# Four edits to a four-layer graph kernel: a copy ahead of its stores, a list spacing, a bias added later, edge sums and rest stores moved

## The chip, the cores and the metric

The kernel runs on one core of a Trainium2 chip. The metric is the time of one execution on the device in microseconds (us), median of three runs. Engines are named as the profile names them: PE (TensorE matmul), PEld (its weight loads), DVE (VectorE), ACT (ScalarE), POOL (GpSimd), SP (SyncE). Each engine carries out its instructions in order, and a DMA is issued by an instruction in the queue of SP, ACT or POOL.

## The reference, cut to what matters

There are 4096 nodes with 256 features and a weighted 4096 x 4096 adjacency, dense in the first rows and columns and thin elsewhere. Four graph layers follow each other, each with a residual and a normalization:

```python
x = layernorm(x + adj @ (x * W))                                   # layer 0
x = layernorm(x + two_steps(x, adj))                               # layer 1
x = layernorm(x + softmax(where(adj != 0, adj * score, -big)) @ x) # layer 2
x = layernorm(x + [x, adj @ x, rowsum(adj * adj.T)] @ weight + bias)  # layer 3
# two_steps: R = (adj + I) / rowsum; twice: A = top-p attention of Xa,
# Xf = R @ Xf, Xa = A @ Xa, Z += Xf @ U1.T + Xa @ U2.T;
# result: layernorm(x + Z) * ln_g + ln_b
```

## The kernel before, in words

A row tile is 128 nodes, so there are 32. The adjacency comes as blocks of 128 x 128. Tiles 0 to 2 are multiplied densely in every layer. For the others layer 0 finds by the way which columns hold anything, and writes a list of them (4 to 7 groups of 128 columns a tile); later layers gather just these rows with indirect DMAs on POOL (L371). In layer 0 itself, tiles 0 to 7 are multiplied densely, and 8 to 31, the 24 listed ones, by their new lists.

**Layer 0** is a loop over slots. In each slot the ends of finished tiles move on by a step (`move_ends`), every second slot multiplies four blocks of a dense tile (`dense_0`, L519, with the maxima that say what is filled, L521), most slots load a quarter of a tile that is to be listed (`find_0`, L528, L531), and then lists and listed products move on by a step each. The order of PE, ACT, DVE and POOL is the order in which the program writes the instructions; SP's own order is left to the scheduler. `list_one` has five steps: counts on DVE (L322 to L325), offsets on PE (L329 to L332, into the bank `lists_ps`), marks on DVE (L338), a product on PE (L342, into the same bank) and the read-out on DVE (L348 to L358). A new list starts at the earliest `APART` slots after the one before.

The end of a tile (`out_0`, seven steps, L447 to L489) normalizes the tile to `xi`, turns it on PE (`xT`), multiplies it for keys and queries (`psq`) and for the residual path (`po`, L442), and then, on ACT, copies keys and queries (`project`, L297 to L302), issues four stores (L475 to L478: `xi` into the tables `tab` and `tak`, and `xb`, which is `xi` plus `ln_b`, made on POOL at L469), copies half of `po` to `qs` (L480) and stores it (L481). `rest` (L485), which DVE does at the end of the slot's dense part, makes `qp` out of the other half of `po` and of `qs`; its store (L489) is the tile's last step.

**Layer 1** has two attention steps over 32 tiles each. Step one follows a written schedule of 15.8 us a tile. Step two has a period of about 32 us a tile; POOL does small operations on one number a row in it, the secant (L757), and gathers for the sums. `out_1` (L1006) ends a tile: load `xb` as `x0` (L1010), scale the sum (L1012), normalize (L1016), times `ln_g` (L1017), plus `x0` (L1018), normalize again (L1023), store `x2`.

**Layer 2** (`product` with `nbr_weights`) goes through 57 chunks: 24 of dense tiles 0 to 2 and 33 pieces of lists, mixed, with the next three chunks of each kind loaded ahead on SP (L1590, L1594). A chunk is weighted on ACT (L1541) and DVE (L1542) and multiplied on PE (L1621). A tile's end, `out_2` (L1646), is spread over the following chunks; it stores y3 on ACT's queue and t3, from a pool of two buffers, on SP's (L1662). Once a chunk the generator `edges_1` (L1560) moves by one `yield`: it loads two 128 x 1024 stretches of `hubs` (512 KB each, L1567) into the upper half of kT, and DVE multiplies them and adds them up (L1569), 12 times in all, for the edge term of tiles 0 to 2. **Layer 3** is the same `product` without weights, reads t3 back (L1672), and adds the edge term in `out_3`.

Of the kernel before, what the change touches and what calls it, by code (L numbers as in the profile page):

```python
# [11 lines left out]
F32 = mybir.dt.float32  # L12
# [6 lines left out]
P = 128  # L19
N = 4096  # L20
D = 256
DA = 64
NT = N // P
# [22 lines left out]
TW = D + DA  # L46
SLOTS = 8
L_EVERY, L_WAIT = 3, 5
F_SLOTS, APART = (6, 7), 3
HB = 8  # L50
NEW = 7
HUBS = (3, 6)
# [22 lines left out]
def gnn_kernel(ctx: ExitStack, tc: tile.TileContext, x, pair, panels, W0, W1, W2T, W3T, U1T, U2T,  # L75
               ln_g, ln_b, Hv, W3L, b3, hubs, out):
    nc = tc.nc
# [5 lines left out]
    dram = ctx.enter_context(tc.tile_pool(name="dram", bufs=1, space=bass.MemoryType.DRAM))  # L83
# [35 lines left out]
    def row_bcast(v, n, name, tag=None):  # L119
        t = const.tile([P, n], F32, name=name, tag=tag or name)  # L120
        nc.gpsimd.dma_start(t, bass.AP(tensor=v.tensor, offset=v.offset, ap=[[0, P], [1, n]]))
        return t

    def one(name, dtype=F32, bufs=2):
        return small.tile([P, 1], dtype, name=name, tag=name, bufs=bufs)

    def rows(I):
        return slice(I * P, (I + 1) * P)
# [3 lines left out]
    w0b, bb = row_bcast(W0, D, "w0b"), row_bcast(ln_b, D, "bb")  # L132
# [104 lines left out]
    def transposed(tiles, name, apart=False):  # L237

        n = 2 * len(tiles)
        pt = bank([P, 4, P], "ptx", "ms")  # L240
        for s, t in enumerate(tiles):
            for h in range(2):
                nc.tensor.transpose(pt[:, 2 * s + h, :], t[:, h * P:(h + 1) * P], ident)
        xT = work.tile([P, 4, P], F32, name=name, tag="xT")
        def turn():
            nc.scalar.copy(xT[:, :n, :], pt[:, :n, :])
        if apart:
            return turn, xT
        turn()
        return xT  # L250
# [23 lines left out]
    def layernorm(o, y, own=True):  # L274
        m, rs = norm_stats(y, own)
        nc.vector.tensor_scalar(o, y, m, rs, op0=OP.subtract, op1=OP.mult)
# [8 lines left out]
    def project(xT, n, I, more=None):  # L285

        half, b = divmod(I, NT // 2)
        r, other = (slice(h * DA, (h + 1) * DA) for h in (half, 1 - half))
        c = rows(n * (NT // 2) + b)
        ps = bank([P, 2, P], "psq", "ms")  # L290
        for h in range(2):
            nc.tensor.matmul(ps[:, 0, :], wqk[:, h, r.start:r.start + P], xT[:, h, :], start=(h == 0), stop=(h == 1))
        if more is not None:
            for h in range(2):
                nc.tensor.matmul(ps[:, 1, :DA], xT[:, h, :], wqk[:, h, :DA], start=(h == 0), stop=(h == 1))
        yield
        nc.scalar.copy(kT[r, c], ps[r, 0, :])  # L297
        q = work.tile([P, P], F32, name="q")
        nc.scalar.copy(q[other, :], ps[other, 0, :])
        (nc.sync if n else nc.scalar).dma_start(qd[n][I], q[other, :])  # L300
        if more is not None:
            nc.scalar.copy(more[:, D:], ps[:, 1, :DA])  # L302

    def run(gen):
        for _ in gen:
            pass
# [110 lines left out]
    tab, tak = (dram.tile([N + P, TW], F32, name=k) for k in ("tab", "tak"))  # L417
    qtab = dram.tile([N, D], F32, name="qtab")
    ttab = dram.tile([N, D], F32, name="ttab")
    qpd, zd, xbd = ([dram.tile([P, D], F32, name=f"{k}_{I}", tag=f"{k}{I}") for I in range(NT)] for k in ("qp", "z", "xb"))  # L420
    x2d = dram.tile([N, D + 2], F32, name="x2d")
    y3d = dram.tile([N, D], F32, name="y3d")
    t3d = dram.tile([N, D], F32, name="t3d")
# [15 lines left out]
    def times_both(xT, u):  # L439
        po = bank([P, 2, D], "po", "ms")  # L440
        for h in range(2):
            nc.tensor.matmul(po.rearrange("p a b -> p (a b)"), xT[:, h, :], u[:, h, :], start=(h == 0), stop=(h == 1))  # L442
        return po
# [3 lines left out]
    def out_0(I, ps, sums, xin):  # L447
        pool = pools["w0"]
        nc.vector.tensor_scalar_add(rone[:, I:I + 1], sums, 1.0)
        nc.vector.reciprocal(rinv[:, I:I + 1], rone[:, I:I + 1])  # L450
        y = pool.tile([P, D], F32, name="y0", bufs=4)
        nc.vector.tensor_mul(y, ps[:, :D], w0b)
        nc.vector.tensor_add(y, y, xin)
        st = small.tile([P, nc.vector.BN_STATS_DIM], F32, name="st")
        nc.vector.bn_stats(st, y)
        mv = small.tile([P, nc.vector.BN_AGGR_DIM], F32, name="mv0", bufs=5)
        nc.vector.bn_aggr(mv, st)
        yield
        rs = one("rs0", bufs=5)
        nc.gpsimd.tensor_scalar_add(rs, mv[:, 1:2], EPS)  # L460
        nc.gpsimd.tensor_tensor(rs, rs, neg_half, OP.pow)
        yield
        xi = pool.tile([P, TW], F32, name="xi", bufs=4)
        nc.vector.tensor_scalar(xi[:, :D], y, mv[:, 0:1], rs, op0=OP.subtract, op1=OP.mult)
        yield
        xT = transposed([xi], "xT0")
        yield
        xb = pool.tile([P, D], F32, name="xb")
        nc.gpsimd.tensor_add(xb, xi[:, :D], bb)  # L469
        qk = project(xT, 0, I, xi)  # L470
        next(qk)
        po = times_both(xT, U[0])
        yield
        run(qk)
        nc.scalar.dma_start(tab[rows(I), :], xi)  # L475
        nc.scalar.dma_start(tak[rows(I), :DA], xi[:, D:])
        nc.scalar.dma_start(tak[rows(I), DA:], xi[:, :D])
        nc.scalar.dma_start(xbd[I], xb)  # L478
        qs = pool.tile([P, D], F32, name="qs")
        nc.scalar.copy(qs, po[:, 1, :])  # L480
        nc.scalar.dma_start(qtab[rows(I), :], qs)  # L481
        qp = pool.tile([P, D], F32, name="qp")

        def rest():
            nc.vector.scalar_tensor_tensor(qp, po[:, 0, :], rone[:, I:I + 1], qs, op0=OP.mult, op1=OP.add)  # L485

        last_of_slot.append(rest)
        yield
        nc.scalar.dma_start(qpd[I], qp)  # L489

    def run_rest():
# [514 lines left out]
    def out_1(a, psa):  # L1006

        I = a["I"]
        x0 = pools["late"].tile([P, D], F32, name="x0")
        nc.sync.dma_start(x0, xbd[I])  # L1010
        h = work.tile([P, D], F32, name="y")
        nc.scalar.activation(h, psa[:, :D], AF.Copy, scale=a["rk"])  # L1012
        yield
        rs, shift = norm_scale(h)
        yield
        nc.scalar.activation(h, h, AF.Identity, scale=rs, bias=shift)  # L1016
        nc.gpsimd.tensor_mul(h, h, gb)  # L1017
        nc.gpsimd.tensor_add(h, h, x0)  # L1018
        yield
        rs, shift = norm_scale(h)  # L1020
        yield
        x2 = pools["late"].tile([P, D + 2], F32, name="x2", tag="o")
        nc.scalar.activation(x2[:, :D], h, AF.Identity, scale=rs, bias=shift)  # L1023
        yield
        nc.vector.scalar_tensor_tensor(h, x2[:, :D], 1.0, hvb, op0=OP.mult, op1=OP.mult, accum_out=x2[:, D + 1:])
        nc.gpsimd.memset(x2[:, D:D + 1], 1.0)
        nc.gpsimd.tensor_copy(scores[:, I:I + 1], x2[:, D + 1:])
        nc.sync.dma_start(x2d[rows(I), :], x2)
# [433 lines left out]
    with tc.manual_schedule(engines=everything):  # L1462
        for I in range(NT + 1):
# [53 lines left out]
            steps(cuts)  # L1517
            run(end)
            end = out_1(at.pop(I), psa) if I < NT else none
            steps(end)  # L1520
            run(cuts)
# [38 lines left out]
    def edges_1():  # L1560

        part = small.tile([P, DENSE, 4], F32, name="part_e", bufs=1)
        half = [kT[:, N // 2:][:, s * CC:(s + 1) * CC] for s in range(2)]
        for I in range(DENSE):
            for c in range(N // CC):
                for t, h in zip(half, hubs):
                    nc.sync.dma_start(t, h[rows(I), c * CC:(c + 1) * CC])  # L1567
                yield
                nc.vector.scalar_tensor_tensor(half[0], half[0], 1.0, half[1], op0=OP.mult, op1=OP.mult,  # L1569
                                               accum_out=part[:, I, c:c + 1])  # L1570
                yield
        nc.vector.tensor_reduce(edge[:, :DENSE], part, AX.X, OP.add)
# [73 lines left out]
    def out_2(I, ps, rk, x2, y3):  # L1646
        y = work.tile([P, D], F32, name="y")
        nc.vector.scalar_tensor_tensor(y, ps[:, :D], rk, x2, op0=OP.mult, op1=OP.add)
        x3 = pools[ends_in[0]].tile([P, D], F32, name="x3", bufs=ends_in[1])
        layernorm(x3, y)  # L1650
        yield
        yield
        turn, xT = transposed([x3], "xT3", True)
        turn()
        yield
        po = times_both(xT, wl)
        yield
        nc.scalar.copy(y3, po[:, 0, :])
        nc.scalar.dma_start(y3d[rows(I), :], y3)
        t3 = pools[ends_in[0]].tile([P, D], F32, name="t3", bufs=-(-ends_in[1] // 2))  # L1660
        nc.vector.tensor_add(t3, x3, po[:, 1, :])
        nc.sync.dma_start(t3d[rows(I), :], t3)  # L1662

    def end_2(I, ps, _):
# [154 lines left out]
```

## Time and profile before

| what | us |
|---|---|
| median of three runs | 2589.42 |
| the three runs | 2587.23 to 2592.84 |
| the profiled execution | 2587.75 |
| its span | 2586.0 |
| busy PE, DVE, POOL, ACT | 2087.2, 2091.6, 1631.2, 1475.9 |
| layer 0 | 0 to about 513 |
| step one | to about 1030 |
| step two | to about 2185 |
| layer 2 | to about 2420 |
| layer 3 | to 2586 |

"Busy" leaves out instructions that only issue a DMA or wait. The profile's table of waits puts idle time of an engine down to what released it. In timelines, each line gives the start, the duration, the engine, the line of the code, the operation, its tiles and sizes, and in brackets the idle time before it with its releaser; ACTq and SPq are the DMA-issuing instructions of ACT and SP.

### The profile page before, as it was taken

The page shows a single profiled execution, that of the slowest core. Times are in us where ns is not written, and L with a number is a line of the kernel's source. Part 1 is how long each engine was busy: PE and PEld are TensorE (multiplying, and loading weights), DVE is VectorE, ACT ScalarE, POOL GpSimd, SP SyncE. Part 2 cuts the span into 40 slices and gives each one's busy share as a digit, 9 for nine tenths or more (in the row PEclk, how much of TensorE's full clock was granted, in tenths as well). Part 3 has the DMA queues.
Part 4 walks back from the last instruction along what each step waited for, and adds up shares of the span by engine and source line. Part 5 has one row for each costly group of instructions (what it writes and reads, how often), then busy time and mean ns, then how long its engine had stood idle before and what let it go on. Part 6 is the DMA issues. An engine that isn't in the chain of part 4 may idle for free.

```text
span 2586.0 us, 36948 instructions
## 1 busy us (share of the span) xinstructions
PE 2087.2 (81%) x10252; PEld 1483.9 (57%) x10252; DVE 2091.6 (81%) x6401; ACT 1475.9 (57%) x2455; POOL 1631.2 (63%) x2720
## 2 busy tenths in 40 slices
PE   4777767689999898869788888888888876679995
PEld 3555445435555555657566666666666665456784
DVE  4788776489999995477799999999999995588587
ACT  0111111168888886557688889999999962234100
POOL 4666544455565656333788887777777773657475
PEclk7888787889999999989899999999999998899997
DMA  9899776435555545645211111111111114987794
GB/s 334 289 309 296 251 250 188 140 107 155 153 161 158 133 129 139 196 131 160 79 58 57 48 45 44 44 43 44 44 45 44 44 57 131 294 248 213 224 299 145
DMA packets 259815, 383.12 MB, mean 148 GB/s; under 512 B 40880, under 2 KB 166336, under 8 KB 259600
## 3 DMA queue, kind: packets, MB, share of 16 engines
q1 hardware_dynamic: 158432, 212.27, 25.5%
q0 software_dynamic: 43664, 124.79, 17.9%
q10 hardware_dynamic: 57504, 43.60, 5.1%
q8 instruction: 84, 1.38, 0.2%
q14 instruction: 131, 1.07, 0.1%
HBM read 321.31 MB, written 59.21 MB: 147 GB/s over the span
## 4 chain that ended last, share of the span: by engine, by line
DVE 25%; PE 16%; ACT 7%; issue 5%; POOL 4%; DMA 3%; SPq 0%; DVEq 0%; ACTq 0%; POOLq 0%
PE acc L1621 5%; PE psa L235 4%; DVE cand L830 4%; DVE e L876 3%; DVE tmp L824 3%; DVE e L872 3%; PE acc L1059 2%; ACT junk L743 2%; DMA kT<-in_hubs 2%; PE lg L633 2%; DVE top L807 2%; DVE rest L809 2%; ACT junk L749 1%; PE pt L224 1%; ACT e L704 1%
## 5 line engine op out<-in xcount | busy, mean ns | idle before, releaser
L235 PE MATMUL psa<-v,eT 128*128 128x256 f32 x2048 | 504.0, 393 | 75.0 <-ACT eT L226 74.5
L235 PEld LDWEIGHTS psa<-v,eT 128*128 128x128 f32 x2048 | 394.6, 197 | 150.5 <-ACT eT L226 96.5
L743 ACT ACTIVATE junk<-e,h 128x4096 bf16<-128x4096 f32 x64 | 237.5, 3710 | 36.8 <-POOL h L723 26.3
L224 PE MATMUL pt<-ident,e 128*128 128x128 f32 x1024 | 157.5, 284 | 100.1 <-DVE e L876 55.1
L749 ACT ACTIVATE junk<-e,h 128x4096 bf16<-128x4096 f32 x62 | 230.8, 3723 | 0.1
L224 PEld LDWEIGHTS pt<-ident,e 128*128 128x128 f32 x1024 | 130.0, 147 | 144.0 <-issue 99.2
L371 POOL DMA_INDIRECT pc<-in_pair,idx_a x130 | 129.0, 992 | 128.4 <-issue 48.6
L830 DVE MAX8 cand<-tmp 128x8 f32<-128x128 f32 x1024 | 203.9, 276 | 1.1
L226 ACT COPY eT<-pt 128x512 f32<-128x512 f32 x256 | 144.9, 588 | 94.2 <-PE pt L224 93.5
L1120 DVE MAX8 cand<-e 128x8 f32<-128x256 f32 x512 | 175.9, 411 | 3.8 <-ACT e L1112 3.6
L371 POOL DMA_INDIRECT xg<-x2d,idx_x x130 | 134.6, 1036 | 69.2 <-PE acc L1621 31.0
L519 PE MATMUL acc<-xw,panel 128*128 128x257 f32 x512 | 156.1, 458 | 25.4 <-DMA panel<-in_panels 14.1
L1150 ACT ACTIVATE marks<-e,mid 128x1024 bf16<-128x1024 f32 x128 | 140.5, 1145 | 39.9 <-DVE mid L1146 35.8
L371 POOL DMA_INDIRECT xg<-ttab,idx_x x130 | 128.7, 990 | 52.8 <-issue 27.5
L371 POOL DMA_INDIRECT xg<-qtab,idx_x x130 | 125.6, 966 | 54.7 <-issue 30.9
L872 DVE SCALAR_TENSOR_TENSOR e<-e,ties 128x1024 f32<-128x1024 f32 x128 | 156.0, 1280 | 3.0 <-DVE ties L868 0.2
L704 ACT ACTIVATE e<-lg 128x1024 f32<-128x1024 f32 x120 | 123.3, 1027 | 52.4 <-PE lg L633 52.4
L824 DVE SCALAR_TENSOR_TENSOR tmp<-e,h 128x2048 f32<-128x2048 f32 x64 | 150.8, 2356 | 2.3
L1109 PE MATMUL lg<-kT,qi 64*128 64x512 f32 x512 | 148.1, 653 | 3.0 <-DVE want L356 2.9
L519 PEld LDWEIGHTS acc<-xw,panel 128*128 128x128 f32 x512 | 116.0, 235 | 58.2 <-issue 32.9
L633 PE MATMUL lg<-kT,qi 64*128 64x512 f32 x480 | 135.5, 641 | 15.6 <-ACT junk L707 15.6
L371 POOL DMA_INDIRECT xg<-y3d,idx_x x111 | 106.6, 960 | 63.7 <-PE acc L1621 41.5
(345 smaller groups left out, 5476.7 us busy)
## 6 DMA issues: line engine op xcount, KB each, us to landing
e<-in_panels SPq DMA_DIRECT2D x96, 512.0 KB
panel<-in_panels SPq DMA_DIRECT2D x136, 256.0 KB
pc<-pk SPq DMA_DIRECT2D x82, 256.0 KB
xg<-ttab SPq DMA_DIRECT2D x96, 128.0 KB
kT<-in_hubs SPq DMA_DIRECT2D x24, 512.0 KB
pc<-in_panels SPq DMA_DIRECT2D x32, 256.0 KB
pc<-pk SPq DMA_DIRECT2D x19, 320.0 KB
tab<-xi ACTq DMA_DIRECT2D x33, 160.0 KB
```

The costliest lines, as they stand in the source:

```text
L224: nc.tensor.transpose(pt[:, k, :], e[:, (g * 4 + k) * P:][:, :P], ident)
L235: nc.tensor.matmul(ps[:, :D], eT[g][:, k, :], rhs[j][:, :D], start=(j == 0), stop=stop and j == NT - 1)
L371: nc.gpsimd.indirect_dma_start(out=o, out_offset=None, in_=src, in_offset=bass.IndirectOffsetOnAxis(ap=idx[:, c], axis=0))
L519: nc.tensor.matmul(ps[:, :D + 1], a[:, k, :], XW[j][:, :D + 1], start=(j == 0), stop=(j == NT - 1))
L633: nc.tensor.matmul(ps[:, h, :], qi[r, :], kT[r, (n * NC + c) * LC:][:, :LC], start=True, stop=True)
L704: nc.scalar.activation(both(e, c), ps, AF.Exp, accum_out=s8[:, c:c + 1])
L743: nc.scalar.activation(junk_tile(), e, AF.Relu, bias=h, scale=-1.0, accum_out=part)
L749: nc.scalar.activation(junk_tile(), e, AF.Sign, bias=h, scale=-1.0, accum_out=below)
L824: nc.vector.scalar_tensor_tensor(w, ec, h, ec, op0=OP.is_lt, op1=OP.mult, accum_out=low[:, c:c + 1])
L830: nc.vector.max(cand[:, c * (NS // 2) + g, :], w[:, g * SEG:(g + 1) * SEG])
L872: nc.vector.scalar_tensor_tensor(eg, eg, ties[:, g:g + 1], eg, op0=OP.is_gt, op1=OP.mult)
L1120: nc.vector.max(a["cand"][:, b, :], a["e"][:, b * SEG0:(b + 1) * SEG0])
```

## The change

In layer 0 ACT copies `qs` straight after the keys and queries, and the stores of `qs` and `xi` follow one step later; `xb` is neither made nor stored, and `APART` goes from 3 to 4. Step two loads `x0` from the first 256 columns of `tab`, whose rows are 320 numbers long, and adds `ln_b` on POOL before the other two POOL operations of that step. In layer 2, `edges_1` waits three chunks instead of one between the loads and the sum, and the store of t3 is issued one step later.

```diff
-F_SLOTS, APART = (6, 7), 3
+F_SLOTS, APART = (6, 7), 4
...
-    qpd, zd, xbd = ([dram.tile([P, D], F32, name=f"{k}_{I}", tag=f"{k}{I}") for I in range(NT)] for k in ("qp", "z", "xb"))
+    qpd, zd = ([dram.tile([P, D], F32, name=f"{k}_{I}", tag=f"{k}{I}") for I in range(NT)] for k in ("qp", "z"))
...
-        xb = pool.tile([P, D], F32, name="xb")
-        nc.gpsimd.tensor_add(xb, xi[:, :D], bb)
         qk = project(xT, 0, I, xi)
         next(qk)
         po = times_both(xT, U[0])
         yield
+        qs = pool.tile([P, D], F32, name="qs")
         run(qk)
+        nc.scalar.copy(qs, po[:, 1, :])
+        qp = pool.tile([P, D], F32, name="qp")
+
+        def rest():
+            nc.vector.scalar_tensor_tensor(qp, po[:, 0, :], rone[:, I:I + 1], qs, op0=OP.mult, op1=OP.add)
+
+        last_of_slot.append(rest)
+        yield
+        nc.scalar.dma_start(qtab[rows(I), :], qs)
         nc.scalar.dma_start(tab[rows(I), :], xi)
         nc.scalar.dma_start(tak[rows(I), :DA], xi[:, D:])
         nc.scalar.dma_start(tak[rows(I), DA:], xi[:, :D])
-        nc.scalar.dma_start(xbd[I], xb)
-        qs = pool.tile([P, D], F32, name="qs")
-        nc.scalar.copy(qs, po[:, 1, :])
-        nc.scalar.dma_start(qtab[rows(I), :], qs)
-        qp = pool.tile([P, D], F32, name="qp")
-
-        def rest():
-            nc.vector.scalar_tensor_tensor(qp, po[:, 0, :], rone[:, I:I + 1], qs, op0=OP.mult, op1=OP.add)
-
-        last_of_slot.append(rest)
-        yield
         nc.scalar.dma_start(qpd[I], qp)
...
-        nc.sync.dma_start(x0, xbd[I])
+        nc.sync.dma_start(x0, tab[rows(I), :D])
...
         nc.scalar.activation(h, h, AF.Identity, scale=rs, bias=shift)
+        nc.gpsimd.tensor_add(x0, x0, bb)
         nc.gpsimd.tensor_mul(h, h, gb)
         nc.gpsimd.tensor_add(h, h, x0)
...
                     nc.sync.dma_start(t, h[rows(I), c * CC:(c + 1) * CC])
-                yield
+                for _ in range(3):
+                    yield
                 nc.vector.scalar_tensor_tensor(half[0], half[0], 1.0, half[1], op0=OP.mult, op1=OP.mult,
                                                accum_out=part[:, I, c:c + 1])
...
         nc.vector.tensor_add(t3, x3, po[:, 1, :])
+        yield
         nc.sync.dma_start(t3d[rows(I), :], t3)
```

## The prediction, made before the changed kernel was run

> **What bounds the kernel now.** First the busy times by stage (window; then its length; busy us and count for PE, PE weight load, DVE, ACT, POOL; granted PE clock; DMA share; GB/s). The windows are layer 0 to 505 us, attention step two from 1135 to 2150, layer 2 in two halves, layer 3.
>
> ```profile
> 0.00:505.00 505.00, 343.66 (x1439) 245.88 (x1439) 355.92 (x870) 57.71 (x238) 273.02 (x458) 0.83 0.82 261
> 1135.00:2150.00 1015.00, 852.93 (x4012) 640.36 (x4010) 923.24 (x2600) 854.41 (x1054) 763.10 (x1580) 0.97 0.20 61
> 2190.00:2300.00 110.00, 75.99 (x258) 53.50 (x259) 71.16 (x217) 38.36 (x123) 71.20 (x68) 0.85 0.89 284
> 2300.00:2410.00 110.00, 101.71 (x386) 70.41 (x385) 92.16 (x327) 49.98 (x162) 63.43 (x62) 0.97 0.73 210
> 2410.00:2586.00 176.00, 141.85 (x615) 117.73 (x613) 129.62 (x473) 1.86 (x5) 106.60 (x111) 0.93 0.71 225
> ```
>
> No engine is full in layer 0; step two is DVE's (91%); the first half of layer 2 does less PE work than the second in the same 110 us, with DMA at 0.89. Next, DVE alone in layer 0:
>
> ```profile
> 60.00:260.00 200.00, 161.77 (x389) 0.87 0.92 300
> 260.00:510.00 250.00, 168.24 (x428) 0.81 0.68 209
> ```
>
> To 260 us DMA (0.92) sets the pace. After that it does not (0.68), and DVE works 168 of 250 us. The waits of that part say where the rest is (engine, line, what it waited for; us, times, longest):
>
> ```profile
> DVE qp L485 <- ACT qs L480: 35.4, 17, 4.9
> DVE rone L449 <- PE acc L566: 32.3, 10, 6.3
> PE lists_ps L329 <- DVE want L356: 17.6, 4, 6.4
> ```
>
> DVE works or waits nearly all of these 250 us (168 + 71), so it is the engine to free. The timeline of one tile's end shows its longest wait being made: ScalarE issues four stores ahead of the copy that DVE stands still for.
>
> ```profile
> 336.27 0.35 ACTq L475 DMA_DIRECT2D tab<-xi  x1
> 336.66 0.44 ACTq L476 DMA_DIRECT2D tak<-xi  x1
> 337.14 0.46 ACTq L477 DMA_DIRECT2D tak<-xi  x1
> 337.70 0.39 ACTq L478 DMA_DIRECT2D xb<-xb  x1
> 338.13 0.37 ACT L480 COPY qs<-po 128x256 f32<-128x256 f32 x1 [1.89 <-DMA tak<-xi]
> 338.53 0.48 DVE L485 SCALAR_TENSOR_TENSOR qp<-po,rone,qs 128x256 f32<-128x256 f32 x1 [1.67 <-ACT qs L480]
> ```
>
> In layer 2 (waits, 2195 to 2300 us) DVE waits for the loads of the edge sums, and PE for the weights that DVE makes behind them:
>
> ```profile
> DVE kT L1569 <- DMA kT<-in_hubs: 26.4, 8, 6.8
> PEld acc L1621 <- DVE pe L1542: 35.9, 12, 7.0
> ```
>
> The chain that ended last agrees: from 2197 to 2286 us most of it is these loads, 5.7 to 8.4 us each, some 50 us in all. Last, step two around the place of the new addition:
>
> ```profile
> 1915.10 0.73 POOL L1017 TENSOR_TENSOR y<-y,gb 128x256 f32<-128x256 f32 x1
> 1921.97 0.25 POOL L848 TENSOR_SCALAR ud<-f_u 128x1 f32<-128x1 f32 x1
> 1924.06 0.29 DVE L868 TENSOR_SCALAR ties<-ties,ud,f_u 128x4 f32<-128x4 f32 x1
> ```
>
> **What the Trainium skill says.** PSUM — Partial Sum Buffer, on bank collisions: accesses of two engines have to be kept apart by bank, not by address. The trace agrees: L329 writes another part of the bank that L356 reads, and waits. DMA: Bandwidth & Descriptors, "Issuing engines are not separate DMA queues": all queues share 16 engines, so a store taken out on ACT's queue is room for SP's loads; here DMA is at 0.92 to 260 us. TensorE: Matmul & The Clock Gate, Part 1: an idle window of about 3.4 us halves the clock, work restores it. In layer 2 eight matmuls take 3.37 us after a 6.7 us wait and 2.00 us otherwise; a removed wait gives a little more than itself.
>
> **The change part by part.** Sums are against the profiled execution, 2587.75 us (span 2586.0, 1.75 around it), which is 1.67 below the median 2589.42.
>
> *Copy ahead of the stores.* From the end of L302 to the copy lie four issues, 1.9 us above, 2.0 at the median tile. I read all 32 tiles: each gains the smaller of DVE's wait and the time by which the copy can start earlier (the later of L302 and PE's po); where po is last, as at 511.9 us, it gains nothing. Out of 50.9 us (24 waits in layer 0) about 31 go. Part of this turns into waits for PE (the 32.3 us above) and for gathers: I count half, -15; ends 5 and 31. The stores now stand at the head of the tile's next step on ACT, whose 58 us of work in 505 leave room; the copy of xT of a later tile can lie up to 2 us behind them, PE waits there already (25 us), which is part of the halving.
>
> *xb left out.* 32 POOL additions of 0.74 us go (24 us, and 9.6 us in which POOL stood still for xi ahead of its gathers), and 32 stores of 131 KB. 13 of these lie before 260 us: 1.7 MB at 300 GB/s is 5.7 us. I take -4, between 0 and -9.
>
> *APART 4.* Counting slots by the loop's rules: both versions take 135. At a spacing of 3 a list's offset matmuls fall into the slot in which the list before it is read out of the same bank, 10 times, at 4 never. The trace has 18.8 us of such waits in 5 cases, with all of PE's queue behind them. But at 4 the next list's counts share a slot with that read-out 19 times instead of 5, and PE waits for counts already (L324, 4.4 us). A third counts: -6, between +5 and -19. Layer 0 together: -25.
>
> *Addition in step two.* 32 POOL additions at 0.73 us (L1017's duration) = 23 us, in POOL's queue ahead of L1017; the x0 load has the same bytes and is issued some 30 us ahead of its use (1916.65 for the next tile). POOL then runs gathers and L848, which DVE needs at L868: 1.84 us of slack above, 1.1 left. Tiles 3 to 6 have two or three gathers more, 1.25 us each, and POOL works without a break: their periods are 33.6 to 34.9 us instead of 32.0. There it counts in full, with one more tile at the edge: 5 x 0.75 = +4; ends 0 and +12 (half of all tiles).
>
> *Edge sums.* A piece took two slots and takes four, 48 of 57 slots. Now 24 slots last 103 us (2195 to 2298), 4.3 each, and the other 33 last 112, 3.4 each. Without the load wait the first part needs PE 75, DVE 63 + gaps, gathers 66 x 1.25 = 83, DMA (30 - 6.3 MB) at 300 GB/s = 79 us; at 91 us it gains 12. The second part takes over 6 sums of 1.31 us on DVE, which is at 92 of 110: +8 if DVE is its bound, 0 if PE; I take +4. Together -8, between -22 and +6. A load has three slots (10 us) for its 7, so no such wait stays.
>
> *Rest stores one slot later.* The same 32 stores on SP, now behind a slot's loads. SP stops waiting for t3 ahead of loads that are three chunks early: 0. The price is that t3 has two buffers: the next-but-one t3 comes 5.8 to 7.2 us after it where ends are close, while the store would be issued some 3.5 us later and land in 2.9 to 4.7. Four ends of 30 are two slots apart, ten three: at most 4 x 3 + 10 x 1 = +20, at least 0; SP's order is not written by hand, so it may not move. I take 0.
>
> Layer 3: nothing. Sum: -25 + 4 - 8 = -29, so 2558.75 profiled, 2560 as a median.
>
> **Rivals.** *Waits only change places in layer 0*: DVE then waits for L566, PE for xT and counts. For: PE has some 80 us of waits there. Against: DVE is hardly ever free. Layer 0 gives -8, the rest -4: 2577. *All of it counts*: -31 - 19 - 9 in layer 0, -18 in layer 2, +4: 2516 at the far end, a likelier 2534. *t3's buffers, slower*: if SP's queue holds the stores back behind loads that wait for buffers (SP's waits for DVE ahead of L1590 and L1594 come to over 100 us), DVE stands still at L1661 in nearly every end. From 1.0 us each (29 / 28 ends) the change gains nothing; at 1.5 us it is +42, 2602. Against: three of four ends are three slots or more apart. *It doesn't do what it says*: SP orders its own queue, and the hub loads may be issued no earlier against the sums; with layer 0 failing as well, no change, 2588.
>
> **Chances.** Forecast 0.58 (2543 to 2575), waits change places 0.17 (2575 to 2584), all counts 0.09 (below 2543), no change 0.06, slower by t3 0.10. The range 2540 to 2584 holds the first two and a third of the next, near 0.8. A measurement of this kernel tells 0.2%, some 5 us, from none: faster 0.84, within 0.06, slower 0.10.
>
> **What would show it.** Right: the wait of L485 for L480 falls from 51 us to about 20; L329's wait for L356 is gone; layer 0 ends near 488 instead of 513 us; L1569 no longer waits for in_hubs and its last sum comes near 2370 us of the old clock; L868's wait for L848 grows in a few early tiles only. Wrong: L449's wait for L566 grows by what L485 loses; L1661 waits for t3d; step two's period leaves 32.0 us.

## The result, and the profile after

| | before | after |
|---|---|---|
| median of four runs, us | 2588.32 | 2555.83 |
| range, us | 2584.34 to 2592.84 | 2554.81 to 2561.94 |
| span of the profiled execution, us | 2586.0 | 2553.7 |

The ratio is 0.9879, with a 95% interval of 0.9856 to 0.9902: 32.5 us faster, where 29 were forecast. To see where the gain comes from, I took the length of each stage from both traces, each stage ending where the last store of its kind is issued (step one: where ACT copies the last `v`):

| stage, ending with | before, us | after, us | difference | forecast |
|---|---|---|---|---|
| layer 0 (`qp`) | 512.8 | 489.6 | -23.2 | -25 |
| step one (`v`) | 524.8 | 522.0 | -2.8 | 0 |
| step two (`x2`) | 1152.0 | 1159.4 | +7.4 | +4 |
| layer 2 (t3) | 230.8 | 221.6 | -9.2 | -8 |
| layer 3 (out) | 159.3 | 156.4 | -2.9 | 0 |

Kernels whose code is the same up to the end of layer 0 differ there by 4.5 and 6.8 us between traces (489.6 and 494.1; 489.5 and 496.3; these kernels come below). So step one and layer 3 show nothing that could be told from no change.

The windows of the profile after, cut at about the same places of the work as in the prediction, have the same columns (window, length, busy us and count of PE, PE weight load, DVE, ACT and POOL, granted PE clock, DMA share, GB/s):

```profile
0.00:490.00 490.00, 344.09 (x1458) 242.12 (x1458) 350.78 (x879) 57.02 (x244) 249.59 (x427) 0.85 0.81 262
260.00:490.00 230.00, 160.28 (x690) 112.86 (x689) 158.24 (x421) 28.63 (x126) 106.60 (x164) 0.84 0.67 211
1115.00:2130.00 1015.00, 848.43 (x3986) 636.15 (x3984) 922.32 (x2596) 852.31 (x1048) 811.66 (x1609) 0.96 0.20 60
```

Layer 0 holds about the same PE and DVE work in 15 us less, and POOL has lost 23 us there (273 to 250), as foreseen. The part behind 260 us is 20 us shorter with the same DMA share. In step two POOL is 49 us busier in this window, of which the additions are 21.8 (30 by 0.727). The rest is in the spans of its operations on one number a row, whose counts are the same; I don't read work from those.

The waits of the second part of layer 0 after (engine, line, what it waited for; us, times, longest) answer to the three lines of the prediction. Lines have moved: L478 was L485, L474 was L480, L563 was L566.

```profile
DVE rone L449 <- PE acc L563: 40.4, 9, 7.7
PE lists_ps L342 <- DVE since L338: 27.6, 12, 2.6
DVE qp L478 <- ACT qs L474: 20.8, 12, 4.8
PE lists_ps L329 <- DVE upto L324: 6.8, 3, 3.3
```

PE no longer waits for the read-out of a list (`want`, L356), and DVE's wait for `qs` fell from 35.4 to 20.8 us; over the whole of layer 0 from 50.9 to 24.9. But DVE's wait for PE at L449 grew from 32.3 to 40.4 (whole layer: 46.9 to 59.4), and PE's for the marks of a list, L338, over the whole layer from 17.8 to 36.1. Taken together, PE's idle time ahead of L329 and L342, the two places where it waits for a list, is 44.6 us before and 44.6 after. So on this chip PE's waits for lists did change places.

DVE's time shows what was gained. Over layer 0 (512.8 and 489.6 us) it was busy for 357.6 us before and 350.4 after, and idle for 155.2 and 139.2. Of the 23.2 us, 16.0 are thus less waiting, and in the other 7.2 DVE does the same work in less time; where these come from is seen below with `xb`.

The timeline of a tile's end (start, duration, engine, line, operation) shows the edit at work: L474 runs at L302's heels, and the stores come behind it.

```profile
318.62 0.21 ACT L302 COPY xi<-psq 128x64 f32<-128x64 f32 x1 [2.92 <-DMA q<-q]
318.73 0.38 ACT L474 COPY qs<-po 128x256 f32<-128x256 f32 x1
...
319.14 0.48 DVE L478 SCALAR_TENSOR_TENSOR qp<-po,rone,qs 128x256 f32<-128x256 f32 x1 [2.74 <-ACT qs L474]
319.53 0.54 ACTq L482 DMA_DIRECT2D qtab<-qs  x1
```

DVE still waits 2.74 us here, no longer for stores, but because ACT itself came late to L302 and what stands ahead of it.

Step two, at one of the tiles with few gathers; `x` is the buffer of `x0`, and L1014 is the new addition:

```profile
1903.61 0.25 POOL L845 TENSOR_SCALAR ud<-f_u 128x1 f32<-128x1 f32 x1
1904.92 0.29 DVE L865 TENSOR_SCALAR ties<-ties,ud,f_u 128x4 f32<-128x4 f32 x1
1927.90 0.73 POOL L1014 TENSOR_TENSOR x<-x,bb 128x256 f32<-128x256 f32 x1
```

From the end of L845 to DVE's need of it are 1.06 us, where 1.84 were before the change: the addition took its 0.73 out of the slack, and DVE does not wait in such a tile. In early tiles it does. DVE's waits in step two, and one of these tiles:

```profile
DVE ties L865 <- POOL ud L845: 26.4, 9, 16.2
```
```profile
1286.72 0.29 DVE L865 TENSOR_SCALAR ties<-ties,ud,f_u 128x4 f32<-128x4 f32 x1 [1.62 <-POOL ud L845]
```

Before it was 22.7 us in 6 waits. In layer 2 the sums no longer wait for their loads (26.4 us before). A small wait of DVE is new there:

```profile
DVE t L1660 <- DMA t3d<-t: 3.9, 2, 2.5
```

It is the one the prediction named as a sign against itself: a t3 waits for the store of the last but one before it, whose buffer it takes.

### The profile page after: what moved, and what is told of

It is laid out like the page before. It is cut to its first block, busy times and chain, and to the rows that moved or that the text cites. A ratio compares the mean times of both kernels' runs of the same rounds, so it can differ in the third digit from the quotient of the medians.

```text
span 2553.7 us, 36818 instructions
## 1 busy us (share of the span) xinstructions
PE 2083.9 (82%) x10252; PEld 1475.9 (58%) x10252; DVE 2085.3 (82%) x6401; ACT 1475.6 (58%) x2455; POOL 1653.3 (65%) x2720
## 3 DMA queue, kind: packets, MB, share of 16 engines
q14 instruction: 130, 1.06, 0.1%
## 4 chain that ended last, share of the span: by engine, by line
DVE 33%; PE 13%; issue 4%; POOL 4%; ACT 4%; DMA 2%; DVEq 0%; SPq 0%; ACTq 0%; POOLq 0%
DVE cand L827 5%; PE psa L235 4%; DVE e L873 4%; DVE tmp L821 4%; DVE e L869 3%; PE acc L1620 3%; PE acc L1057 2%; DVE top L804 2%; DVE rest L806 2%; DVE vt L267 1%; PE pt L224 1%; ACT junk L740 1%; PE lg L630 1%; POOL xg L371 1%; DMA t3d<-t 1%
## 5 line engine op out<-in xcount | busy, mean ns | idle before, releaser
L516 PE MATMUL acc<-xw,panel 128*128 128x257 f32 x512 | 148.5, 441 | 25.0 <-DMA panel<-in_panels 13.2
L701 ACT ACTIVATE e<-lg 128x1024 f32<-128x1024 f32 x120 | 123.0, 1025 | 48.9 <-PE lg L630 48.8
L1110 ACT ACTIVATE e<-lg 128x1024 f32<-128x1024 f32 x128 | 130.5, 1020 | 29.2 <-PE lg L1107 28.5
```

The costliest lines, as they stand in the source:

```text
L516: nc.tensor.matmul(ps[:, :D + 1], a[:, k, :], XW[j][:, :D + 1], start=(j == 0), stop=(j == NT - 1))
```

## The experiments

The theory to test was the prediction's: layer 0 gains by the copy (most), the spacing and `xb`; step two pays for five tiles; layer 2 gains by the edge sums, and the later store of t3 is free. The rivals were that the waits of layer 0 only change places, and that the late t3 store costs time.

The experiments ran on three chips, each beside the kernel before, and the chips are not alike. The kernel before took 2910.1 us on chip A (all kernels named `only_`), 2890.75 on chip B (`undo_apart`, `undo_copy`, `undo_t3`, `split_add`) and 2589.28 on chip C (`undo_xb`, `rest_last`, `best`, `best_rest`). The runs shown above, with 2588.32, are like those of chip C; whether it is the same chip is not known, and "the faster chip" means both. On A and B step one takes 754 to 780 us instead of 525, with DVE idle and no local engine as releaser (the trace of `only_edges` puts 108 us down to "remote" at one line). What makes it so was not found. Step two lasts about the same there (1154.0 on A, with its code as before), layer 0 537.4 instead of 512.8, layer 3 186 to 189 instead of 159. So stage lengths are compared below, within a chip where nothing else is said. There is one trace of each kernel.

### Layer 0: each edit alone

`only_copy`: the copy ahead, with all the stores, that of `xb` too, one step later.

```diff
-        nc.scalar.dma_start(tab[rows(I), :], xi)
-        nc.scalar.dma_start(tak[rows(I), :DA], xi[:, D:])
-        nc.scalar.dma_start(tak[rows(I), DA:], xi[:, :D])
-        nc.scalar.dma_start(xbd[I], xb)
         nc.scalar.copy(qs, po[:, 1, :])
-        nc.scalar.dma_start(qtab[rows(I), :], qs)
...
         yield
+        nc.scalar.dma_start(qtab[rows(I), :], qs)
+        nc.scalar.dma_start(tab[rows(I), :], xi)
...
```

> The kernel before with the copy of qs ahead of its stores alone; the stores, that of xb among them, go out one step later. If a removed wait of DVE counts by half, layer 0 (512.8 us before, its last qp store) ends 15 us earlier and the whole is 15 us shorter. If waits only change places, layer 0 gains under 5 us and DVE's wait for PE at L449 (46.9 us) grows by what its wait for qs loses (50.9 before). Either way the wait for qs falls to some 20 us and later stages keep their lengths within 2 us.

`only_apart`:

```diff
-F_SLOTS, APART = (6, 7), 3
+F_SLOTS, APART = (6, 7), 4
```

> The kernel before with a list spacing of 4 slots alone. If PE's waits for the shared bank lie on the path by a third, layer 0 is 6 us shorter; L329's wait for L356 (18.8 us) goes to 0. If the waits only move to the next list's counts (L324, 4.4 us before), layer 0 changes by less than 3 us and that wait grows by 10 or more.

`only_xb`: the addition moved to step two and the store left out, nothing else.

```diff
-        nc.gpsimd.tensor_add(xb, xi[:, :D], bb)
-        nc.scalar.dma_start(xbd[I], xb)
...
-        nc.sync.dma_start(x0, xbd[I])
+        nc.sync.dma_start(x0, tab[rows(I), :D])
+        nc.gpsimd.tensor_add(x0, x0, bb)
```

> The kernel before with xb left out of layer 0 and ln_b added on POOL in step two. Forecast: layer 0 4 us shorter (32 stores and 24 us of POOL work less; the copy of qs also loses one of the four issues ahead of it), step two 6 to 7 us longer in its first nine tiles, where POOL has no idle time, so about +3 in all. If the gain of layer 0 came mainly from bytes on the DMA engines and from POOL, layer 0 is 12 us shorter or more.

`only_edges`: the edge sums alone; its layer 0 is that of the kernel before, so it is also the layer 0 that the others are held against.

```diff
-                yield
+                for _ in range(3):
+                    yield
```

> The kernel before with three chunks instead of one between the loads of the edge sums and the sum. If the whole of the gain of layer 2 is this edit, its chunks are 9 to 12 us shorter in all: the first 24 some 21 us faster, the other 33 slower by some 9 (six sums of 1.3 us on a busy DVE), and a bit better than with t3 stored later, whose buffer waits (3.9 us) are absent. If the store of t3 has a part in it, the gain is under 5 us.

| kernel | median, us | ratio (95%) | layer 0, us | against 537.4 | forecast | DVE busy, idle there |
|---|---|---|---|---|---|---|
| `only_copy` | 2888.65 | 0.9925 (0.9906 to 0.9943) | 522.2 | -15.2 | -15 | 357.7, 164.5 |
| `only_apart` | 2890.55 | 0.9926 (0.9907 to 0.9945) | 514.0 | -23.4 | -6 | 354.3, 159.7 |
| `only_xb` | 2913.08 | 1.0009 (0.9990 to 1.0027) | 527.1 | -10.3 | -4 | 350.4, 176.7 |
| `only_edges` | 2902.64 | 0.9973 (0.9958 to 0.9987) | 537.4 | | | 359.3, 178.1 |

In layer 0 the copy gave what was forecast, and the spacing, the change of a single digit, four times its forecast. In the medians of all runs the two are alike, 21.5 and 19.6 us below the kernel before. Here are waits in layer 0 of `only_edges`, then of `only_copy`, then of `only_apart`:

```profile
PE lists_ps L329 <- DVE want L356: 23.8, 7, 6.4
DVE qp L485 <- ACT qs L480: 40.2, 18, 6.1
```
```profile
DVE qp L480 <- ACT qs L476: 21.3, 12, 5.8
```
```profile
PE lists_ps L329 <- DVE upto L324: 5.9, 5, 2.1
```

The copy halves its own wait and hardly touches the other (20.0 us are left of the 23.8). In `only_apart` the wait for `want` is gone. The prediction had reckoned that two thirds of it would come back as waits for counts; that wait (L324) is 5.9 us, hardly more than the 4.4 of the trace it was read from. Yet half of it did come back, elsewhere: PE's idle time ahead of L342 is 44.1 us instead of 31.7. That the stage lost 23.4 us, about what the wait took, is thus no proof that the wait counted in full. These are all of layer 0 in `only_edges` and in `only_apart`:

```profile
0.00:537.40 537.40, 361.86 (x1458) 255.58 (x1458) 359.26 (x874) 59.61 (x244) 271.58 (x459) 0.80 0.77 247
0.00:514.00 514.00, 343.06 (x1458) 243.40 (x1458) 354.28 (x874) 59.56 (x244) 274.66 (x459) 0.83 0.80 258
```

PE's idle time fell by 5 us only (175.5 to 170.9); its same 1458 matmuls took 19 us less, at a granted clock of 0.83 instead of 0.80. DVE's idle time fell by 18 us. So the spacing spares DVE waits and PE slow work, but by what path the one digit does it is not shown.

`xb` gains 10.3 us in layer 0, and 8.9 of them are DVE's own work, which is the same 874 instructions. The cause shows in the single instructions: beside an addition for `xb` on POOL an instruction of DVE takes longer. L464, which makes `xi`, before and after (shortest, median and longest of 32 in ns):

```profile
L464 DVE TENSOR_SCALAR xi<-y,mv,rs x32: 380/406/999, 71.8 to 504.7; 128x256 f32<-128x256 f32 x32
L464 DVE TENSOR_SCALAR xi<-y,mv,rs x32: 381/406/568, 70.1 to 480.8; 128x256 f32<-128x256 f32 x32
```

The longest, 999 ns at 400.88 us, overlaps the addition that starts at 401.63. In all, the 60 DVE instructions that overlap these additions before take 6.1 us more than the median of their kind. In the five traces with `xb` in layer 0 DVE is busy for 354.3 to 359.3 us there, in the nine without it for 350.0 to 351.3. Step two shows no such thing: the 84 DVE instructions that overlap the new additions there take no longer than their median. Which instructions are slowed, and why, is open.

Step two gives 4.3 us of the 10.3 back (1158.3 against 1154.0). The two stages would leave a gain of 6 us, but over all its runs the total of that kernel is that of the kernel before.

### Layer 0: one edit taken back

`undo_apart` is the changed kernel with `APART` at 3; `undo_copy` has the stores ahead of the copy again; `undo_xb` makes and stores `xb` in layer 0 and has no addition in step two.

> The changed kernel with the list spacing back at 3 slots. Alone, the spacing gave 21 us of the whole and the copy 22, the two together with xb left out no more than 23 in layer 0 of the changed kernel. If the two free the same stretches (DVE and PE stand still in turn in the same slots), layer 0 is only 4 to 10 us longer than in the changed kernel of this call (undo_t3, split_add). If each is worth in company what it is worth alone, it is 20 us longer. L329's wait for the list's read-out is back at about 20 us.

> The changed kernel with three stores ahead of the copy of qs again (xb stays out). If the edits overlap, layer 0 is 4 to 10 us longer than in undo_t3 and split_add; if they add up, 15 us. DVE's wait for qs rises by 15 to 25 us.

> The changed kernel with xb made and stored in layer 0 again (its store with the other late ones) and no addition in step two. Alone, leaving xb out gave 10 us in layer 0 and cost 4 in step two, the whole being the same. If that holds in company, layer 0 is 8 to 12 us longer than 492 and step two 7 us shorter than 1162, so the whole is within 5 us of the changed kernel. If only the bytes count (forecast: 4 us), layer 0 is 3 to 5 us longer and the kernel with xb is the faster one by 3.

| kernel | median, us | ratio to before (95%) | layer 0, us | the changed code on that chip |
|---|---|---|---|---|
| `undo_apart` | 2874.29 | 0.993 (0.991 to 0.995) | 514.6 | 492 |
| `undo_copy` | 2863.51 | 0.990 (0.986 to 0.994) | 509.3 | 492 |
| `undo_xb` | 2558.85 | 0.9896 (0.9871 to 0.9920) | 501.2 | 489.6 |

(492 is from `undo_t3` and `split_add` below, 491.4 and 492.5, which have the changed layer 0.) Taking the spacing back costs 22.6 us and the copy 17.4, about as much as each gave alone; in the medians it is 22 to 23.5 us and 11.5 to 13 against the same two kernels. If the edits freed the same stretches, taking one back would have cost less than it gave alone, as the expectations above have it. It doesn't: on these chips the three edits add up, 15.2 + 23.4 + 10.3 = 49 alone against 537.4 - 492 = 45 together (two chips, so a rough sum). PE's wait for `want` is back in `undo_apart`, 16.3 us in 5 waits.

On the faster chip the whole of layer 0 fell by 23.2 us only. `undo_xb` is 11.6 us longer there than the changed kernel, but 7.1 longer than `best`, whose layer 0 is the same code. DVE's work is the steadier measure: 357.3 us with `xb` and 350.4 and 350.0 without, so about 7 us are `xb`'s. Some 11 to 16 stay for copy and spacing, and how these divide was not measured. (The step two of `undo_xb` is 9.5 us shorter than the changed kernel's, 1149.9 us, so that the totals differ by 3 us only.) So the slower chips show that each edit works, and not how much each gives on the faster one.

### Layer 0: what holds the rest

`rest_last` moves `rest` (the `qp` of a tile, L478) from the end of the dense part to the end of the slot, so that DVE comes to it later and ACT has more time.

```diff
-            run_rest()
             for g in list(active):
...
                 started = n
+            run_rest()
```

> The changed kernel with DVE's product of qs and po (rest) at the end of the slot, behind the lists' work, instead of behind the dense part. If DVE's remaining wait for qs (17 to 25 us in layer 0) is on the path like the part removed, it falls under 8 us and layer 0 is 8 to 15 us shorter than 492. If the engine behind it is bound elsewhere by now (DVE's wait for PE at the tile's sums, 37 to 59 us), that wait takes over and layer 0 keeps its length within 3 us.

It took 2554.82 us, 0.9880 (0.9852 to 0.9908), as the changed kernel. Its waits in layer 0:

```profile
DVE rone L449 <- PE acc L563: 62.9, 17, 8.4
DVE qp L478 <- ACT qs L474: 13.0, 10, 2.3
```

DVE's wait for `qs` is halved once more, from 24.9 to 13.0, but layer 0 stays at 489.5 us. DVE's idle time is 138.4 us after 139.2: its wait for PE at L449 rises from 59.4 to 62.9, and one for the product of a list (L348) from 0.7 to 6.5. This time the waits do change places. But the edit also brings a wait of its own, PE's for L478 to leave the bank of `po` (8.1 us in 4 cases, none after the change). So it shows that this edit gains nothing, and not that what is left of the wait for `qs` is free.

### Step two: how many tiles have no slack

`split_add` gives the new addition to DVE in tiles 0 to 9, and leaves it on POOL in the others.

```diff
-        nc.gpsimd.tensor_add(x0, x0, bb)
+        (nc.vector if I < 10 else nc.gpsimd).tensor_add(x0, x0, bb)
```

> The changed kernel with ln_b added on DVE instead of POOL for the first ten tiles of step two. If these tiles are bound by POOL, their periods (33.1 to 35.6 us) fall by about 0.7 us each to those of the kernel before, and step two is 5 to 7 us shorter than in undo_t3. If DVE is their bound, they get 0.4 us longer each, 4 us in all.

Its total, 2850.81 us, 0.9870 (0.9824 to 0.9915), can't be told from that of `undo_t3` on the same chip (2852.01). But step two lasts 1155.5 us against 1162.3. The periods from tile to tile say where, taken from the starts of DVE's last operation on a tile (L1025 before, L1023 after). For the pair of traces shown above the first ten were

```
before  48.60 34.87 33.76 33.62 33.76 32.65 32.00 32.32 32.29 32.56, then 32.00
after   48.59 35.58 34.34 34.36 34.34 33.08 33.14 33.20 33.17 32.81, then 32.00
```

Nine tiles, not five, are longer by 0.25 to 1.14 us, 6.2 us in all. Their number and order fit tiles 3 to 11, which gather more than four groups of columns. In `split_add` the periods of the tiles with six groups are back at 33.7, those with five at 32.3 to 33.2. (The tile with seven has 36.3 there, but on chip A 36.2 to 36.4 without any addition as well.) So the tiles with five gathers, which I had taken to have room because their period was near 32.0, were at the edge: with 0.73 us more POOL is late in them too.

### Layer 2: the edge sums, and the store of t3

`only_edges` above has the edge sums alone, on chip A. From the start of DVE's first weighting of a chunk (L1542) to the 25th it takes 99.6 us there, against 107.3 to 109.4 in the three other kernels of that chip: 8 to 10 us less, where its expectation had 21. The rest of the chunks takes 124.3 us, against 117.2 to 124.7. All of layer 2 is 241.7 us, against 242.4, 248.4 and 252.0 in kernels whose layer 2 is the code before. So the code before alone spreads over 10 us there, and only the first part and the total (0.9973, 7.5 us) show a gain on that chip. Why it is less than half of that on the faster chip, below, was not found.

`undo_t3` has t3 and its store in one step, as before; `best` has this and `split_add` in one, and `best_rest` has `rest_last` as well.

```diff
         nc.vector.tensor_add(t3, x3, po[:, 1, :])
-        yield
         nc.sync.dma_start(t3d[rows(I), :], t3)
```

> The changed kernel with the store of t3 in the same step as t3. If its delay is worth nothing, layer 2 keeps its length within 3 us, with DVE's wait at t3 for its store (3.9 us in the changed kernel) gone. If the delay had helped SP's loads, layer 2 is 5 us or more longer. Layers 0 and 1 are those of the changed kernel.

> The changed kernel with t3 stored at once and ln_b added on DVE for the first ten tiles of step two. From the two alone: step two 6.8 us shorter, layer 2 unchanged within 3, so 5 to 8 us shorter in all than the changed kernel; about 0.985 of the kernel before.

> The same two and rest at the end of the slot. If rest_last gains in layer 0, this is the fastest kernel of the study, 15 us below the changed kernel; if it does not, it equals best within 3 us.

First, what the step does. SP's order is not the program's, and few stores moved. From the start of a t3 to the issue of its store are 0.52 us at the median in the changed kernel, and 0.52 before. Seven stores of 32 are issued after 0.8 to 1.0 us and one after 2.5; before, one after 0.85 and one after 2.2. The prediction had 3.5 us for all.

`undo_t3`: 2852.01 us, 0.9876 (0.9829 to 0.9923), layer 2 246.0 us, against 244.2, 242.8 and 248.6 in `undo_apart`, `undo_copy` and `split_add`: on that chip, nothing gained. On the faster chip it is otherwise. Layer 2 lasts 211.2 us in `best` and 211.0 in `best_rest`, which have the store in t3's own step, and 221.6, 221.4 and 218.2 in the changed kernel, `rest_last` and `undo_xb`, which have it one step later. `best` and `best_rest` differ from the changed kernel in step two as well, and the store alone was not put back on that chip. The windows hold the first 24 chunks of layer 2, in which the edge sums used to be, and the next 32 of the other 33, for the changed kernel and then for `best`:

```profile
2174.40:2256.82 82.42, 68.90 (x248) 49.14 (x248) 60.98 (x196) 37.12 (x119) 63.19 (x64) 0.91 0.92 289
2256.82:2377.56 120.74, 106.33 (x380) 72.53 (x380) 98.27 (x333) 49.57 (x162) 66.24 (x66) 0.93 0.78 244
```
```profile
2177.70:2257.05 79.35, 66.69 (x248) 47.93 (x248) 60.87 (x197) 36.99 (x119) 60.63 (x62) 0.93 0.91 298
2257.05:2370.49 113.44, 100.04 (x380) 68.53 (x380) 97.72 (x334) 49.59 (x162) 70.32 (x68) 0.98 0.81 262
```

Before, the two parts took 103.9 and 108.5 us. With t3 stored in its own step the edge sums thus give -24.5 and +4.9; the changed kernel has 3.1 and 7.3 us more. Of the 7.3, 6.3 are PE's own: the same 380 matmuls take 106.33 us at a granted clock of 0.93 instead of 100.04 at 0.98. PE does not wait longer for that: it is idle for 14.4 and 13.4 us, with four waits of over 2 us in both, the longest 3.4. But in the changed kernel the clock is halved four times in this part, for 17 us, and in `best` once, for 3.4. One place where the store shows in the changed kernel's timeline, with SP's loads between a t3 and its store left out:

```profile
2323.84 0.42 DVE L1660 TENSOR_TENSOR t<-x,po 128x256 f32<-128x256 f32 x1
2324.85 1.06 SPq L1662 DMA_DIRECT2D t3d<-t  x2
2325.14 0.41 DVE L1660 TENSOR_TENSOR t<-x,po 128x256 f32<-128x256 f32 x1
...
2333.20 0.42 DVE L1660 TENSOR_TENSOR t<-x,po 128x256 f32<-128x256 f32 x1 [2.46 <-DMA t3d<-t]
```

Two ends lie 1.3 us apart, both buffers are taken, the stores go out as a pair behind two loads of 512 KB, and the third t3 stands 2.46 us for the first of them, with DVE's queue behind it. In `best` the same two ends lie 1.3 us apart too, but the first store goes out between the two loads, and the third t3 waits 0.7 us. Such waits are 3.9 us in the changed kernel, 7.6 in `rest_last`, 6.8 in `undo_xb`, 0.7 in `best`, 0.8 in `best_rest` and none before. They don't account for all of the difference: `undo_xb` has 6.8 us of them, and PE's clock is 0.99 in the second part there. So five traces on the faster chip part by 7 to 10 us along the place of the store, but that the store is the cause is not shown: few stores moved, the clock has a large share, one chip shows nothing, and step two differs as well. A third buffer for t3 was not tried.

`best` takes 2548.15 us, 0.9841 (0.9820 to 0.9862), and `best_rest` 2543.71, 0.9826 (0.9803 to 0.9848), the fastest. Both are ahead of the changed kernel's 0.9879, with 10.4 us less in layer 2 and 3 to 7 us less in step two, and with 5 to 7 us more in layer 0. The 4.4 us between the two can't be put down to `rest`: layer 0 is 494.1 and 496.3 us in them.

## Why the prediction was right, and where its steps were off

The sign and the size were right: 29 us were forecast, and the profiled execution lost 32.2. The mechanisms for the copy and the edge sums were right too. But four terms were off, in both directions, and that they came to 29 in sum is in part luck.

**Copy, -15.** Right where it could be seen alone (-15.2), and by its own mechanism: the wait for `qs` fell from 50.9 to 24.9 us in the changed kernel, about 20 were foreseen. (The 2.0 us that it reads from L302 to the copy at the median tile are 2.2 over all 32 tiles, which changes nothing.)

**Spacing, a third counts, -6.** The wait for the read-out went, as foreseen, but the share was wrong: alone the spacing gave 23.4 us on a slower chip. The argument for a third was that counts and read-outs would meet more often at 4; the wait for counts was 4.4 us before and 8.5 after. What grew instead was PE's wait for the marks (17.8 to 36.1 us). Why the stage gained more than PE's waits did is open, and what the spacing gives on the chip of the forecast was not measured. On PSUM — Partial Sum Buffer, on bank collisions, the Trainium skill has accesses guarded by bank and not by address; the trace agrees as far as it goes: PE's wait for a read-out of another part of the bank, 18.8 us before, is none after.

**xb, -4 in layer 0.** Also too small: -10.3 alone, 7 to 12 on the faster chip. The prediction counted bytes of DMA and POOL's idle time. What it has no term for is that POOL's addition slows DVE beside it: 8.9 of the 10.3 us, and about 7 on the faster chip, are DVE's same work done in less time. But moved work is not removed work: step two took back 4.3 and 9.5, and the edit as a whole is worth nothing that can be measured (1.0009 alone, 2558.85 against 2555.83 us without it).

These three, added up on the slower chips, are about 45 to 49 us, where 25 were forecast; on the chip of the forecast they gave 23.2. The sum was right there, while the division within it was shown wrong only on the others. The rival "waits only change places" is refuted for the copy and the spacing on the slower chips. On the faster one it is true of PE's waits for lists (44.6 us before and after) and of a further step with `qs` (`rest_last`); DVE's idle time fell by 16 us there all the same.

**Step two, five tiles, +4.** Nine tiles, +6.2 in the periods and +7.4 in the stage; within the range of 0 to 12. The step that failed was to read slack from a tile late in the loop (1.84 us) and a period near 32.0 as room.

**Edge sums, +12 gained and 4 given back, -8.** The stage shows -9.2, but as a difference of terms that were off. In `best` the first part gained 24.5 us, where 12 were forecast: it came down to 79.4 us, which is where the prediction's own bounds for gathers (83 us for 66; 62 lie in this window) and DMA (79) lie. I had taken 91. The second part lost 4.9, as forecast. On chip A the first part gained 8 to 10 us only, so the bounds were not reached there.

**t3's later store, 0.** The prediction's own upper bound for it, 4 x 3 + 10 x 1, is 22 and not 20. Layer 2 of the changed kernel is 10 us longer than that of `best`, so 0 may be wrong, but the cause is not shown. The rival had DVE stand still in nearly every end, for 29 us or more; it did in 2 ends, for 3.9 us. What both had wrong is the premise: the store was not issued some 3.5 us later but, at the median, when it was before. "SP's order is not written by hand, so it may not move" was the part that held.

**The clock.** The prediction took from TensorE: Matmul & The Clock Gate, Part 1 of the Trainium skill that an idle window of about 3.4 us halves the clock. The trace does not need a whole one: three of the four halvings in the second part of the changed kernel came behind waits of 2.1 to 2.2 us, and PE had worked for 1.0 to 1.3 us of the 3.4 us before each of the four. The same page says that these windows run on by themselves, whenever the work starts, which fits that of four such waits in `best` only one was followed by a halving. So a wait of PE can cost more than itself or not, and 6.3 us between two kernels may be where their waits fell.

## What to carry to other kernels

Look for instructions that a copy stands behind in its own queue, and put the one that another engine waits for first. Compare the busy time of the same instructions before and after: an edit on one engine can slow the work of another. Where the program does not set the order of a queue, look in the trace whether an edit moved anything. An operation moved to another stage has to be priced tile by tile there, and a period near its floor is no proof of room. A total that comes out right says little about its terms: of layer 0's forecast, one term was a quarter of what it gave alone and one less than half.

## What was not expected of the hardware

The same kernel took 2588 us on one chip, 2891 on a second and 2910 on a third, most of it in step one (525 us, against 775 in `only_edges` on the third, whose step one is the same code), and the gain of one edit to layer 0 (the spacing, 23.4 us) was on a slower chip as large as that of the whole change to layer 0 on the faster one. And POOL's additions of 0.74 us slowed DVE's instructions beside them in layer 0, one from 0.41 to 1.00 us, while additions of the same kind slowed none in step two.
